# Six residual buffers, a closing norm in four pinned steps, and a bias added by an accumulating DMA

## The chip, the cores and the metric

The kernel runs on one core of a Trainium2 chip. A core has a matrix engine (TensorE, "PE" in the profile, with its weight loads as "PEld"), a vector engine (VectorE, "DVE"), an engine for activation functions (ScalarE, "ACT"), a general engine (GpSimd, "POOL"), and a queue engine that only issues DMAs (SyncE, "SP"). Each takes its own instructions in a fixed order and waits on semaphores for the others. The metric is the time of one execution on the device, in microseconds (us); lower is better.

## The reference

Two layers work on x of 32 examples of 512 rows of 256 columns, with a 512x512 adjacency matrix for each example. All arithmetic is float32.

```python
x = x + L0_gnn(layernorm(x), adj)
x = x + L0_ffn(layernorm(x))
x = x + L1_gnn(layernorm(x), adj)
x = x + L1_ffn(layernorm(x))

def L0_ffn(x):                       # 1024 features
    t = max over d of (x[:, d] + Wt[:, d]) + bt
    trop = s * max_k(t*sl_cvx + of_cvx) + (1-s) * min_k(t*sl_ccv + of_ccv)
    g = sigmoid(x @ Wg + bg)
    return (g * trop + (1-g) * gelu(x @ Wc + bc)) @ Wd + bd

def L1_gnn(x):                       # 4 heads of 64 columns
    h = x @ W
    att = softmax(leaky_relu(e_src + e_dst), masked by adj)
    out = relu(att @ h + bias) + h
    return (out - mean) / sqrt(var + 1e-6) * gamma + beta     # per head

def L1_ffn(x):                       # 8 heads, 64 slices
    sw = softmax((x @ W_x.T) @ W_slice.T / temperature)
    st = weighted means of x @ W_fx.T over the slices sw
    ot = a short two-directional scan over the 64 slice tokens, gated, RMS-normed
    return (ot spread back by sw) @ out_w.T + out_b
```

## The kernel before

The program is written for a scheduler. The source traces instructions in some order; the scheduler then simulates the program and gives each engine's instructions an order of their own: a later instruction that the simulation finds ready sooner can be put ahead of an earlier one. What it puts in an engine's queue is then fixed. `tc.keep_in_program_order(ins)` adds one edge to this: `ins` is not put ahead of the instruction that was traced just before it on the same engine. It adds no wait on the chip.

**Layer 0** (`layer0_sorted`, L98) runs from the start to about 2390 us. `convs` does the graph convolution, example by example. `feed_forwards` (L543) works on groups of 512 rows (32 groups in all): `sums` (L546) gathers the rows of a group with indirect DMAs (`xs`, L553), fetches rows of a table (`best`, L564; `rows`, L595) and takes their running maximum on VectorE (L598); `mixed` (L613) does the two matrix products with gelu and tanh and the piecewise linear parts; `down` (L645) multiplies by Wd and adds to `xg` (L654). At the end of `sums`, POOL adds the last bias `bd`, a constant of 128x256 in SBUF, to the four row tiles of `xg` (L609 to L610). The indirect DMAs are issued by POOL, from the same queue of instructions.

**Layer 1** (`layer1_plain`, L865) runs from there to the end. Two chains of Python generators are interleaved by hand:

- `attentions` (L1300): for each example b, `attention(b)` woven with `prepare(b + 1)`. `prepare` (L1136) loads the residual rows `x` with four indirect DMAs (L1142), issues the adjacency copy for b+2 (L1085), norms and transposes them, multiplies by W (`hp`, L1171), and makes `hv`, `mine`, `other` and `ht` from the product (L1174 to L1179). `mine` is turned by a TensorE transpose (`minep`, L1183) and goes through DRAM to every partition (`own`). `attention` (L1204) walks 8 turns of (head pair, row tile), weighs ahead of itself on VectorE (`att`, L1201) and multiplies on TensorE (`avp`, `adp`); it then divides, adds a bias by an accumulating DMA (L953) and leaves a generator `norm` (L1274) in `unfinished`. The steps of `norm` of example b are taken inside the turns of example b+1, at L1245. Its last step adds to the residual (L1296) and marks the example `attended`.
- `mixer(g)` (L1565), for pairs of examples: `slices` of both (softmax rows `sw`, products `yTp`, L1310), `tokens`, `scan` (L1375: a long chain of small products and vector work), and `unslice` (L1554: `outp`, and the store of the result, L1562).

The driver (L1581) steps the mixer; each yield of the mixer carries a number, which times `PACE` gives the number of attention steps to take next. If an attention step yields True, `prepare` is blocked, and the saved-up credit is dropped. `slices(b)` takes attention steps by itself for as long as b is not `attended`. `prepare(b)` is blocked until example b - `AHEAD_X` is stored, since the residual tile `x` has `AHEAD_X` buffers; it is held from `prepare` to `unslice`. `TURNS`, `STEPS` and `WANTED` count the yields of an attention, of `prepare`, and of a mixer's numbers.

All biases of layer 1 are kept in DRAM (`added`) and added by accumulating DMAs from POOL (`add_rows`, L951).

Of the kernel before, what the change touches and what calls it, by code (L numbers as in the profile page):

```python
# [8 lines left out]
F32 = mybir.dt.float32  # L9
# [5 lines left out]
ALU = mybir.AluOpType  # L15
# [4 lines left out]
P = 128  # L20
# [77 lines left out]
def layer0_sorted(tc, ident, eps, x, adj, w, x2s, ranks, over, following):  # L98
# [29 lines left out]
    with ExitStack() as ctx:  # L128
# [11 lines left out]
        bias = const("bias", [P, D], w["bias"].partition_broadcast(P))  # L140
        bd = const("bd", [P, D], w["bd"].partition_broadcast(P))
        wc = cst.tile([P, DC, FFN], F32, tag="wc", name="wc")
# [31 lines left out]
        for c in range(CT // P):  # L174
            nc.gpsimd.affine_select(below[:, c, :], below[:, c, :], pattern=[[1, CT]], compare_op=ALU.is_gt,
                                    fill=0.0, base=-c * P, channel_multiplier=-1)

        table = dr.tile([D, FFN], F32, tag="table", name="table", bufs=1)
        least = dr.tile([2, D], F32, tag="least", name="least", bufs=1)
# [363 lines left out]
        def feed_forwards():  # L543


            def sums(s, g):  # L546
# [57 lines left out]
                for c in range(DC):  # L604
# [3 lines left out]
                                        ALU.is_gt)  # L608
                for t in range(NT):  # L609
                    nc.gpsimd.tensor_add(xg[:, t, :D], xg[:, t, :D], bd)  # L610
                got[s, g] = xg, xnT, best
# [253 lines left out]
def layer1_plain(tc, ident, eps, x2s, ranks, adj, w, out, over, ps):  # L865
# [22 lines left out]
    AP = AH // 2  # L888
    TURNS = AP * NT + 6
    STEPS = 11  # L890
    WANTED = 68
    AHEAD = 3
    ATT = 2 * (AHEAD + 2) + AP + 1
    HW = P // AH
    AHEAD_X = 2 * GB + 1
    PACE = 1.04 * GB * (TURNS + STEPS) / WANTED

# [3 lines left out]
    with ExitStack() as ctx:  # L901
# [234 lines left out]
        def prepare(b):  # L1136
# [29 lines left out]
            other = sb.tile([P, NT, AH], F32, tag="other", name=f"other{b}")  # L1166
            mine = sb.tile([P, AH, NT], F32, tag="mine", name=f"mine{b}")
            for t in range(NT):
                ph = psum("any", f"hp{b}_{t}")
                for c in range(DC):  # L1170
                    nc.tensor.matmul(ph[:, : AH * (HO + 2)], xnT[:, c, t * P : (t + 1) * P], wa[:, c, :],  # L1171
                                     start=c == 0, stop=c == DC - 1)
                d = ph[:, AH * HO : AH * HO + AH]
                nc.scalar.activation(hv[:, t, :, HO], d, AF.Exp)  # L1174
                nc.vector.tensor_mul(hv[:, t, :, :HO], ph[:, : AH * HO].rearrange("p (h e) -> p h e", h=AH),
                                     hv[:, t, :, HO:].to_broadcast([P, AH, HO]))
                nc.scalar.activation(mine[:, :, t], ph[:, AH * (HO + 1) : AH * (HO + 2)], AF.Exp, scale=1.0 - SLOPE)
                nc.scalar.activation(other[:, t, :], d, AF.Exp, scale=SLOPE - 1.0)
                nc.scalar.copy(ht[:, t, :], ph[:, : AH * HO])  # L1179
                yield  # L1180

            pt = psum("any", f"minep{b}")
            nc.tensor.transpose(pt[: AH * NT, :P], mine.rearrange("p h t -> p (h t)"), ident)  # L1183
            row = sb.tile([AH * NT, P], F32, tag="turned", name=f"turned{b}", bufs=1)
# [19 lines left out]
        def attention(b):  # L1204
# [21 lines left out]
            for i, (q, j) in enumerate(turns):  # L1226
# [17 lines left out]
                yield  # L1244
                if unfinished and i not in (0, 3):  # L1245
                    next(unfinished[0], None)
                    yield
                    if i > 3:
                        unfinished.pop()
# [24 lines left out]
        def norm(b, av):  # L1274

            _, ht, _, _, _ = ready[b]
            xt = xs[b]
            NG = NT * AH
            flat = av.rearrange("p t h e -> p (t h e)")
            rows = av.rearrange("p t h e -> p t (h e)")  # L1280
            heads = av.rearrange("p t h e -> p (t h) e")
            nc.vector.scalar_tensor_tensor(flat, flat, 0.0, ht.rearrange("p t e -> p (t e)"), ALU.max, ALU.add)
            mu = sb.tile([P, 2, NG], F32, tag="mu", name=f"mu{b}")
            nc.vector.tensor_reduce(mu[:, 0, :], heads, AX.X, ALU.add)
            nc.vector.tensor_scalar_mul(mu[:, 0, :], mu[:, 0, :], 1.0 / HO)
            nc.vector.tensor_sub(heads, heads, mu[:, 0, :].unsqueeze(2).to_broadcast([P, NG, HO]))
            sq = ht.rearrange("p t (h e) -> p (t h) e", e=HO)
            nc.scalar.activation(sq, heads, AF.Square)
            yield
            nc.vector.tensor_reduce(mu[:, 1, :], sq, AX.X, ALU.add)  # L1290
            nc.vector.tensor_scalar(mu[:, 1, :], mu[:, 1, :], 1.0 / HO, 1e-6, ALU.mult, ALU.add)
            nc.gpsimd.tensor_tensor(mu[:, 1, :], mu[:, 1, :], eps[:, 1:2].to_broadcast([P, NG]), ALU.pow)  # L1292
            nc.vector.tensor_mul(rows, rows, gamma.unsqueeze(1).to_broadcast([P, NT, AH * HO]))
            yield
            nc.vector.tensor_mul(heads, heads, mu[:, 1, :].unsqueeze(2).to_broadcast([P, NG, HO]))
            nc.vector.tensor_add(xt, xt, rows)  # L1296
            del ready[b]
            attended.add(b)
# [76 lines left out]
        def scan(g, uT):  # L1375
# [161 lines left out]
            rms = sb.tile([P, GB], F32, tag="rms", name=f"rms{g}")  # L1537
            nc.vector.tensor_scalar(rms, pm[:, :GB], 1.0 / DI, LN_EPS, ALU.mult, ALU.add)
            nc.gpsimd.tensor_tensor(rms, rms, eps[:, 1:2].to_broadcast([P, GB]), ALU.pow)
# [691 lines left out]
```

## Time and profile before

| What | Value |
|---|---|
| Runs, median of 3 (lowest to highest) | 4513.17 us (4503.5 to 4514.52) |
| The profiled execution, its own time | 4515.02 us |
| Its span, first to last instruction | 4513.3 us |
| Mean granted TensorE clock | 0.94 |
| Busy, VectorE | 3204.0 us of the span |
| `bd` additions L610, POOL | 128, 108.2 us, mean 850 ns |
| `av<-added` L953, POOL's time to issue | 32, 28.1 us, mean 878 ns |
| Closing norm, L1282, L1284, L1286, L1293, L1295, L1296 (VectorE) | 32 of each, 1.21 to 1.23 us each |
| Power of the closing norm, L1292 (POOL) | 32, mean 3.18 us |
| Square of the closing norm, L1288 (ScalarE) | 32, mean 1.06 us |
| Gathered rows `x`, L1142 (POOL) | 128, mean 1.03 us to issue |

How to read it: busy time says how full an engine is, idle time that ends on a releaser says what it waited for. In the views of waits a line names the waiting engine, tile and line, the engine, tile and line that released it, the total in us, how often, and the longest. In a timeline a line gives the start, the length, the engine, the line of the source, the operation, the tiles, and in brackets the idle time of the engine just before and what ended it. Averages over the whole span mix two layers with different limits, so the stretch of the layer in question is looked at by itself.

### The profile page before, as it was taken

The page shows a single profiled execution, that of the slowest core. Times are in us where ns is not written, and L with a number is a line of the kernel's source. Part 1 is how long each engine was busy: PE and PEld are TensorE (multiplying, and loading weights), DVE is VectorE, ACT ScalarE, POOL GpSimd, SP SyncE. Part 2 cuts the span into 40 slices and gives each one's busy share as a digit, 9 for nine tenths or more (in the row PEclk, how much of TensorE's full clock was granted, in tenths as well). Part 3 has the DMA queues.
Part 4 walks back from the last instruction along what each step waited for, and adds up shares of the span by engine and source line. Part 5 has one row for each costly group of instructions (what it writes and reads, how often), then busy time and mean ns, then how long its engine had stood idle before and what let it go on. Part 6 is the DMA issues. An engine that isn't in the chain of part 4 may idle for free.

```text
span 4513.3 us, 56135 instructions
## 1 busy us (share of the span) xinstructions
PE 3933.4 (87%) x19799; PEld 2468.0 (55%) x19799; DVE 3204.0 (71%) x6909; ACT 2198.0 (49%) x4305; POOL 1570.2 (35%) x2069
## 2 busy tenths in 40 slices
PE   5567898899988999889997999898998898989987
PEld 4454565656656656555553555555555455555555
DVE  6678888897788877867765766656666666666663
ACT  3345565556565665545663444344444443444433
POOL 2356544664446554444313122222211222222110
PEclk8778999999999999989998999999999999999998
DMA  5546543664446643564315233333322333333210
GB/s 129 160 142 224 184 140 110 206 202 154 135 129 206 194 141 109 169 216 160 129 59 117 52 76 79 80 80 68 83 68 62 73 80 80 80 70 76 62 38 20
DMA packets 301248, 524.04 MB, mean 116 GB/s; under 512 B 104823, under 2 KB 180227, under 8 KB 300956
## 3 DMA queue, kind: packets, MB, share of 16 engines
q0 software_dynamic: 117120, 383.06, 30.6%
q1 hardware_dynamic: 183836, 137.30, 10.4%
q8 instruction: 158, 2.59, 0.2%
q14 instruction: 134, 1.10, 0.1%
HBM read 463.11 MB, written 73.95 MB: 119 GB/s over the span
## 4 chain that ended last, share of the span: by engine, by line
PE 32%; DVE 31%; DMA 15%; issue 9%; POOL 8%; ACT 4%; SPq 1%; DVEq 0%; POOLq 0%; ACTq 0%
DVE acc L637 4%; PE clsp L623 4%; PE po L652 4%; DMA av<-added 3%; PE yTp L1339 3%; PE gatep L623 3%; PE outp L1559 3%; POOL mu L1292 2%; DMA rows<-table,xs 2%; DMA out<-x 2%; DMA rows<-table,tops 2%; DVE best L598 2%; PE oTp L1527 2%; DVE att L1201 2%; PE avp L1237 2%
## 5 line engine op out<-in xcount | busy, mean ns | idle before, releaser
L623 PE MATMUL clsp<-xnT,wc 128*128 128x512 f32 x1024 | 524.8, 631 | 46.7 <-ACT cls L625 34.4
L623 PE MATMUL gatep<-xnT,wg 128*128 128x512 f32 x1024 | 496.8, 605 | 9.3 <-ACT gate L625 9.3
L652 PE MATMUL po<-wd,acc 128*128 128x256 f32 x2048 | 457.3, 382 | 8.4 <-DVE acc L641 5.9
L652 PEld LDWEIGHTS po<-wd,acc 128*128 128x128 f32 x2048 | 389.2, 192 | 75.2 <-issue 9.6
L1201 DVE SCALAR_TENSOR_TENSOR att<-own,other,mask 128x512 f32<-128x512 f32 x512 | 358.3, 737 | 12.8 <-DMA own<-ownd 12.8
L598 DVE SCALAR_TENSOR_TENSOR best<-rows,xs,best 128x1024 f32<-128x1024 f32 x212 | 272.6, 1288 | 126.8 <-ACT best L592 79.5
L637 DVE SCALAR_TENSOR_TENSOR acc<-past,fld,acc 128x512 f32<-128x512 f32 x448 | 344.6, 772 | 23.8 <-ACT past L636 16.0
L1237 PE MATMUL avp<-att,hv 128*32 128x512 f32 x2048 | 333.0, 601 | 7.2 <-DVE att L1201 7.2
L1339 PE MATMUL yTp<-sw,x 128*128 128x512 f32 x512 | 262.1, 666 | 88.0 <-DVE sw L1334 88.0
L623 PEld LDWEIGHTS gatep<-xnT,wg 128*128 128x128 f32 x1024 | 196.8, 196 | 253.3 <-issue 203.5
L632 ACT ACTIVATE acc<-tz,fld 128x512 f32<-128x512 f32 x256 | 198.7, 776 | 279.1 <-PE tz L630 247.4
L636 ACT ACTIVATE past<-tz,fld 128x512 f32<-128x512 f32 x448 | 291.5, 693 | 79.3 <-DVE acc L637 77.7
L595 POOL DMA_INDIRECT rows<-table,xs x212 | 251.5, 1186 | 170.3 <-DVE best L598 117.3
L623 PEld LDWEIGHTS clsp<-xnT,wc 128*128 128x128 f32 x1024 | 183.9, 200 | 185.9 <-issue 114.1
L434 PE MATMUL pm<-h,adj 128*128 128x258 f32 (+1 forms) x1024 | 182.9, 326 | 103.9 <-DVE keep L427 42.6
L1327 PE MATMUL lgp<-wsl,x4T 128*128 128x512 f32 x512 | 241.3, 617 | 22.4 <-ACT x4T L1131 22.4
L625 ACT ACTIVATE gate<-gatep,fld 128x512 f32<-128x512 f32 x256 | 175.4, 685 | 146.4 <-PE gatep L623 124.0
L553 POOL DMA_INDIRECT xs<-rows_of,order x128 | 156.7, 1225 | 215.3 <-DVE acc L637 93.3
L1339 PEld LDWEIGHTS yTp<-sw,x 128*128 128x128 f32 x512 | 104.9, 214 | 227.5 <-DVE sw L1334 126.2
L1559 PE MATMUL outp<-v,swT 128*128 128x256 f32 x1024 | 226.2, 379 | 0.0
L434 PEld LDWEIGHTS pm<-h,adj 128*128 128x128 f32 x1024 | 152.8, 215 | 129.2 <-issue 73.4
L625 ACT ACTIVATE cls<-clsp,fld 128x512 f32<-128x512 f32 x256 | 176.0, 687 | 95.3 <-PE clsp L623 58.8
(593 smaller groups left out, 8550.7 us busy)
## 6 DMA issues: line engine op xcount, KB each, us to landing
adj<-in_adj POOLq DMA_DIRECT2D x128, 256.0 KB
x<-added POOLq DMA_DIRECT2D x64, 512.0 KB
own<-ownd SPq DMA_DIRECT2D x128, 256.0 KB
rows_of<-keep SPq DMA_DIRECT2D x32, 550.0 KB
x<-in_x SPq DMA_DIRECT2D x32, 512.0 KB
x2s<-xs SPq DMA_DIRECT2D x32, 512.0 KB
short<-in_adj POOLq DMA_DIRECT2D x32, 512.0 KB
av<-added POOLq DMA_DIRECT2D x32, 512.0 KB
```

What stands on the lines that cost most here:

```text
L434: nc.tensor.matmul(pm[:, : c1 - c0], a[:, i, t * P : (t + 1) * P], h[:, i, c0:c1], start=i + c0 == 0, stop=i + 1 == NT and c0 > 0)
L595: nc.gpsimd.indirect_dma_start(out=row, out_offset=None, in_=table, in_offset=bass.IndirectOffsetOnAxis(ap=idxs[:, k : k + 1].bitcast(U32) ...
L598: nc.vector.scalar_tensor_tensor(m, row, vals[:, k : k + 1], m, ALU.add, ALU.max)
L623: nc.tensor.matmul(pf, wf[:, c, f * P : (f + 1) * P], xnT[:, c, :], start=c == 0, stop=c == DC - 1)
L625: nc.scalar.activation(o, pf, fn, bias=fld[:, f, bf : bf + 1], scale=1.0 if fn == AF.Gelu else 0.5)
L636: nc.scalar.activation(r, z, AF.Relu, bias=fld[:, f, AT + b : AT + b + 1])
L637: nc.vector.scalar_tensor_tensor(y, r, fld[:, f, CH + b : CH + b + 1], y, ALU.mult, ALU.add)
L652: nc.tensor.matmul(po[:, i, :], acc[f][:, t * P : (t + 1) * P], wd[:, f, :], start=f == 0, stop=f == FC - 1)
L1201: nc.vector.scalar_tensor_tensor(e, own[h], other[:, j, h : h + 1], mask[:, j, :], ALU.max, ALU.mult)
L1237: nc.tensor.matmul(pv[p][k * HW : (k + 1) * HW, :], hv[:, j, h, e : e + HW], weighed[b, h, j], **ends)
L1339: nc.tensor.matmul(py, xn[:, t, c * P : (c + 1) * P], sw[:, t, :], start=t == 0, stop=t == NT - 1)
L1559: nc.tensor.matmul(po[:, :D], swT[:, k, t * P : (t + 1) * P], v[:, k, :], start=k == 0, stop=k == KC - 1)
```

## The change

- `AHEAD_X` is 2 * GB + 2 = 6 instead of 5: a sixth buffer for the residual tile, and `prepare(b)` is blocked only until b - 6 is stored.
- `norm` has four steps instead of three: the square on ScalarE is a step of its own. The steps are taken after turns 1, 2, 3 and 6 of the next example, where the three steps were taken after turns 1, 2 and 4. Four of its instructions, the first of each step on its engine, are kept in program order. `TURNS` counts one more.
- In `scan` there is one more yield before `rms`, and `rms` is kept in program order. `WANTED` counts one more.
- In `prepare`, the product of `hv` on VectorE reads the copy `ht` in SBUF instead of the PSUM tile, and is traced one row tile later. The transpose of `mine` is kept in program order.
- In layer 0, `bd` lives in DRAM, repeated for the four row tiles, and is added to a group's rows by one accumulating DMA from POOL instead of four POOL additions. The SBUF constant is gone.

```diff
-        bd = const("bd", [P, D], w["bd"].partition_broadcast(P))
...
+        bd = dr.tile([NT, D], F32, tag="bd", name="bd", bufs=1)
+        nc.sync.dma_start(bd, w["bd"].partition_broadcast(NT))
...
-                for t in range(NT):
-                    nc.gpsimd.tensor_add(xg[:, t, :D], xg[:, t, :D], bd)
+                nc.gpsimd.dma_start(xg[:, :, :D], bd.partition_broadcast(P), accum_op=ALU.add)
...
-    TURNS = AP * NT + 6
+    TURNS = AP * NT + 7
     STEPS = 11
-    WANTED = 68
+    WANTED = 69
...
-    AHEAD_X = 2 * GB + 1
+    AHEAD_X = 2 * GB + 2
...
+            def values(t):
+                nc.vector.tensor_mul(hv[:, t, :, :HO], ht[:, t, :].rearrange("p (h e) -> p h e", h=AH),
+                                     hv[:, t, :, HO:].to_broadcast([P, AH, HO]))
+
             for t in range(NT):
...
                 nc.scalar.activation(hv[:, t, :, HO], d, AF.Exp)
-                nc.vector.tensor_mul(hv[:, t, :, :HO], ph[:, : AH * HO].rearrange("p (h e) -> p h e", h=AH),
-                                     hv[:, t, :, HO:].to_broadcast([P, AH, HO]))
                 nc.scalar.activation(mine[:, :, t], ph[:, AH * (HO + 1) : AH * (HO + 2)], AF.Exp, scale=1.0 - SLOPE)
                 nc.scalar.activation(other[:, t, :], d, AF.Exp, scale=SLOPE - 1.0)
                 nc.scalar.copy(ht[:, t, :], ph[:, : AH * HO])
+                if t:
+                    values(t - 1)
                 yield
 
+            values(NT - 1)
+
             pt = psum("any", f"minep{b}")
-            nc.tensor.transpose(pt[: AH * NT, :P], mine.rearrange("p h t -> p (h t)"), ident)
+            tc.keep_in_program_order(
+                nc.tensor.transpose(pt[: AH * NT, :P], mine.rearrange("p h t -> p (h t)"), ident))
...
-                if unfinished and i not in (0, 3):
+                if unfinished and i in (1, 2, 3, 6):
                     next(unfinished[0], None)
                     yield
                     if i > 3:
...
-            nc.vector.scalar_tensor_tensor(flat, flat, 0.0, ht.rearrange("p t e -> p (t e)"), ALU.max, ALU.add)
+            tc.keep_in_program_order(
+                nc.vector.scalar_tensor_tensor(flat, flat, 0.0, ht.rearrange("p t e -> p (t e)"), ALU.max, ALU.add))
...
             sq = ht.rearrange("p t (h e) -> p (t h) e", e=HO)
-            nc.scalar.activation(sq, heads, AF.Square)
-            yield
-            nc.vector.tensor_reduce(mu[:, 1, :], sq, AX.X, ALU.add)
+            yield
+            tc.keep_in_program_order(nc.scalar.activation(sq, heads, AF.Square))
+            yield
+            tc.keep_in_program_order(nc.vector.tensor_reduce(mu[:, 1, :], sq, AX.X, ALU.add))
             nc.vector.tensor_scalar(mu[:, 1, :], mu[:, 1, :], 1.0 / HO, 1e-6, ALU.mult, ALU.add)
             nc.gpsimd.tensor_tensor(mu[:, 1, :], mu[:, 1, :], eps[:, 1:2].to_broadcast([P, NG]), ALU.pow)
             nc.vector.tensor_mul(rows, rows, gamma.unsqueeze(1).to_broadcast([P, NT, AH * HO]))
             yield
-            nc.vector.tensor_mul(heads, heads, mu[:, 1, :].unsqueeze(2).to_broadcast([P, NG, HO]))
+            tc.keep_in_program_order(
+                nc.vector.tensor_mul(heads, heads, mu[:, 1, :].unsqueeze(2).to_broadcast([P, NG, HO])))
             nc.vector.tensor_add(xt, xt, rows)
...
             rms = sb.tile([P, GB], F32, tag="rms", name=f"rms{g}")
-            nc.vector.tensor_scalar(rms, pm[:, :GB], 1.0 / DI, LN_EPS, ALU.mult, ALU.add)
+            yield 1
+            tc.keep_in_program_order(
+                nc.vector.tensor_scalar(rms, pm[:, :GB], 1.0 / DI, LN_EPS, ALU.mult, ALU.add))
```

## The prediction

> **What bounds the kernel now.** I read the page first, then the engines' busy time over layer 1's steady stretch, then TensorE's waits there, then all waits and the timelines of one period.
>
> The page's first part says TensorE is the fullest engine, but not full:
>
> ```profile
> PE 3933.4 (87%) x19799; PEld 2468.0 (55%) x19799; DVE 3204.0 (71%) x6909; ACT 2198.0 (49%) x4305; POOL 1570.2 (35%) x2069
> ```
>
> Layer 1's mixer repeats every 129.9 us (the first `yTp` of a pair of examples starts at 3268.41 and the next pair's at 3398.27). Over 14.2 such periods, from 2500 to 4340 us (columns: length, busy time of PE, PEld, DVE, ACT, POOL, clock, DMA share, GB/s):
>
> ```profile
> 2500.00:4340.00 1840.00, 1674.99 (x10525) 988.58 (x10527) 1194.32 (x2744) 794.32 (x1862) 384.07 (x416) 0.96 0.33 73
> ```
>
> TensorE idles 1840.0 - 1675.0 = 165 us, 11.6 a period, and nothing else is above 65%. So the stage is bound by TensorE plus the waits that end on it. These are, in the same stretch (us, times, longest):
>
> ```profile
> PE yTp L1339 <- DVE sw L1334: 87.4, 21, 7.5
> PE lgp L1327 <- ACT x4T L1131: 21.5, 15, 3.4
> PE minep L1183 <- ACT mine L1177: 17.1, 14, 1.3
> PE oTp L1527 <- ACT yT L1521: 10.2, 14, 0.7
> PE yp L1509 <- DVE mix L1502: 8.4, 13, 0.6
> ```
>
> More than half is one stall a period: TensorE waits for the softmax rows `sw`. Why they are late is read in the timeline of POOL and VectorE, 3376 to 3395:
>
> ```profile
> 3383.88 1.06 POOL L1142 DMA_INDIRECT x<-x2s,ranks  x1 [3.84 <-DMA out<-x]
> ...
> 3389.30 2.96 POOL L1292 TENSOR_TENSOR mu<-mu,eps 128x16 f32<-128x16 f32 x1
> ```
> ```profile
> 3392.30 1.22 DVE L1295 TENSOR_TENSOR av<-av,mu 128x1024 f32<-128x1024 f32 x1 [9.53 <-POOL mu L1292]
> ```
>
> The row loads of an example ahead (L1142) wait for the output store that frees their buffer. The power of the closing norm (L1292) stands behind them on POOL though its input was ready at 3381.4. VectorE stands at L1295 for 9.53 us with the sixteen `sw` instructions of the next example behind it. TensorE runs dry at 3391.1. Over 2600 to 4300 us the same kind of stall, an engine standing at an instruction fed late by another, shows as:
>
> ```profile
> ACT ht L1288 <- DVE av L1286: 317.6, 27, 20.7
> ACT mine L1177 <- DVE hv L1175: 148.5, 27, 12.1
> ```
> ```profile
> DVE av L1295 <- POOL mu L1292: 151.2, 27, 9.9
> DVE rms L1538 <- PE msp L1535: 92.9, 13, 7.9
> ```
>
> These do not add up on the path; they say which instructions stand in front of others.
>
> [...] after the 6.12 us stall before 3268.41 the granted clock is 0.50 until past 3272, and those sixteen `yTp` matmuls take 9.28 us against 7.21 for the sixteen at 3297.99. A long stall costs 2.07 us more than itself. [...] L598 takes 1.28 us alone and 1.58 to 1.75 beside POOL's two-input additions. [...]
>
> **The change part by part.** The sum is against the profiled execution, 4515.0 us (span 4513.3); the median of the runs, 4513.2, is 1.8 lower, so results are moved by that.
>
> 1. *Six residual buffers.* The buffer of example b is free once b-6 is stored, not b-5. Now b=17 needs the store of 12 and b=18 that of 13, both just made; with six, 17's is a period old and 18's is the first of the pair. L1142's waits (59.4 us, 26 times) should go. Two things follow. POOL reaches L1292 earlier: four loads at 1.25 us and the adjacency copy 0.61 are 5.6 us from 3375, so the power could run from 3381.4 instead of 3389.3, 7.9 us sooner. And the hand-written interleave is no longer stopped: a blocked `prepare` yields True and sets the credit to zero, so attention steps meant for the scan are now pushed in a lump ahead of the next `slices`. x += rows (L1296) ends at 3330.15 and its reader begins at 3330.73: no lead at all. Six buffers let up to one example of lead grow.
> 2. *Norm in four steps, `rms` after a yield, both pinned.* No instruction is added. L1288, L1295 and L1538 are queued behind what was traced before them; in the trace that is attention multiplications (0.74 us each) and `sw` work that was ready. What is behind a pinned instruction still waits for it, but for less. The price: the last quarter moves from turn 4 to turn 6, later by two turns, four L1201 x 0.74 = 3.0 us of VectorE and 24 matmuls, about 2.6 us. Cover is the lead of part 1.
>    Parts 1 and 2 together: the `yTp` stall is 6.2 us a period (87.4/14); in the period above VectorE was free from 3382.8 and the rows take 7.7 us (3265.05 to 3272.78 one period earlier), so nearly all can go. I take 5.0 x 14 = 70, and of the clock's 2.07 x 14 = 29 I take 24. With L1288 no longer holding ACT (18.8 us at 3377, the `x4T` copies behind it), `lgp`'s 21.5 gives 12.
> 3. *`values` from `ht`, one tile later.* Four VectorE products per example move from PSUM to SBUF; L1175 is 0.42 us and no SBUF row of that shape is in the trace, but L639 (both in SBUF, 0.70 for 512 columns) against L1265 (one in PSUM, 0.68) says the same price: 128 x 0.02 = under 3 us either way, hidden in VectorE's 35% idle. ACT's `mine` no longer waits for it, and with the pinned transpose `minep` (17.1) I take 12.
> 4. *New waits and the end.* A denser queue gets stalls of its own; the trace can't show them. Bounds 0 and 4 us a period (then the gain is mostly given back); I take 1.5 x 14 = 21. More lead ends attention sooner, so more of the mixer at the end runs without filler: there it idles 4.29 + 5.73 us already before 4376. I take 10.
> 5. *Layer 0's bias.* Out: 128 POOL additions of 0.85 us, 108.2. In: 32 accumulating DMAs; `av<-added` issues in 0.88, so 28 us of POOL. Net 80 us of POOL's 1120 there; POOL isn't the bound. Relief for VectorE: L637's mean is 0.772 against 0.74 undisturbed, 0.03 x 448 = 14 us, and L598's excess about 11; if 40% is L610's, 10 us. Against it: 32 x 512 KB more through POOL's queue (4.4% of its 383 MB). `av<-added` takes 5.2 us to land; gathers behind it are late by 0 to 5.2. At 1436 us two gathers took 10.08 us with the DMA engines full and TensorE idle for 5.19, so it is not always covered. Behind the DMA's own wait for the last `xn` read stand gathers as well; the additions waited there too (190 us, 43 times). Bounds -25 and +166; I take +10 for traffic, -10 for VectorE: 0. The constant's own move is one 4 KB copy, covered by the 301 us before its first use (L610's first start).
>
> Sum: 70 + 24 + 12 + 12 = 118 gained, 21 + 10 given back: 87. 4515.0 - 87 = 4428; as a median 4426.
>
> **Rivals.**
> - *The interleave gains more:* the lead fills the scan's bubbles as well (`oTp`, `yp`, `rnp`: 25 us) and no new waits come: 118 + 21 = 139, so 4374 to 4390; take 4385. For it: 165 us of idle and no other full engine. Against: those bubbles are single-chain waits of 0.6 us.
> - *Nothing to tell (4513):* the stall is only moved, the power's chain (3.3 us on POOL after a DMA) sets the period wherever it stands. Against: its input was ready 7.9 us before it ran.
> - *Slower, the late quarter:* if the lead doesn't grow (pace 4% above need), each `slices` starts 3.0 us later with no cover: 32 x 3.0 = 96, and the `yTp` stall stays. With `minep` and `lgp` gained: 4513 + 96 - 24 = 4585. It decides once the quarter's delay exceeds the buffer's gain; the 0.6 us between L1296 and its reader speak for it, the unblocked `prepare` against.
> - *Slower, layer 0's queue:* the accumulating DMA in front of gathers, in full: 166 - 87 = +79, 4592. It flips the sign from 2.7 us a group. Its transfer is real; most gathers have four buffers of lead against it.
>
> **How the numbers follow.** Forecast 0.55 (its own range 4395 to 4465), gains more 0.20, nothing 0.07, late quarter 0.10, layer 0 0.08. About 0.3%, 13.5 us, is what can be told from no change here. Faster 0.75, same 0.07, slower 0.18. The range from 4370 to 4540 leaves out the far part of the two slower cases and a little below.
>
> **What would show it.** Right: no L1142 wait for the store; L1295's and L1538's waits under a third; `yTp`'s under 25 us; sixteen `yTp` at 7.2; TensorE above 94% in the steady stretch; a period near 123 us; layer 0 ending within 15 us of before. Wrong: L1296 directly ahead of its reader still, `lgp` or `yTp` waits as before; ACT waiting at L1164 for a later reduction; gathers or POOL standing at the new DMA, layer 0 longer.

## The result and the profile after

The change makes the kernel barely faster: 4500.77 us median of 20 runs (4490.82 to 4519.19) against 4510.6 us of the kernel before on the same chips (4495.61 to 4527.49, 20 runs). The ratio is 0.998, with a 95% interval of 0.9971 to 0.999. The forecast was 4426.

The busy times of the kernel after, on its page:

```profile
PE 3943.5 (88%) x19799; PEld 2480.2 (55%) x19799; DVE 3180.0 (71%) x6909; ACT 2199.5 (49%) x4308; POOL 1515.7 (34%) x1973
```

Where the 19.6 us between the two profiled spans (4513.3 and 4493.7) come from is read from the first and last start of two tiles, `po` (the end of layer 0) and `outp` (layer 1's last product):

| Stretch | Before | After | Difference |
|---|---|---|---|
| Start to the last `po` of layer 0 | 2386.3 | 2356.2 | -30.1 |
| From there to the first `outp` | 202.5 | 211.1 | +8.6 |
| First `outp` to last `outp` | 1914.9 | 1914.4 | -0.5 |
| Last `outp` to the end | 9.6 | 12.0 | +2.4 |

So layer 0, where nothing was expected, gives all of the gain, and layer 1, where 87 us were expected, gives none: from the last `po` to the end it takes 2127.0 us before and 2137.5 after. The stretch from 2500 to 4340 us of the kernel after (length, busy time of PE, PEld, DVE, ACT, POOL, clock, DMA share, GB/s), and TensorE's largest waits in it:

```profile
2500.00:4340.00 1840.00, 1695.90 (x10575) 1008.26 (x10574) 1209.20 (x2737) 796.61 (x1849) 389.38 (x406) 0.96 0.33 71
```
```profile
PE yTp L1530 <- DVE y L1525: 30.2, 14, 2.3
PE yTp L1350 <- DVE sw L1345: 28.5, 34, 2.4
PE yp L1520 <- DVE mix L1513: 16.9, 14, 1.5
PE gp L1490 <- ACT cpad L1465: 14.0, 12, 1.2
PE yTp L1350 <- ACT sw L1339: 13.7, 3, 5.5
PE oTp L1538 <- ACT yT L1532: 9.4, 14, 0.7
PE qp L1504 <- ACT ht L1182: 9.4, 12, 1.1
```

The long stall for `sw` went from 87.4 to 42.2 us (28.5 + 13.7), and `lgp`'s wait from 21.5 to 3.1. In their place the scan waits: for `y` (30.2, new), `yp` twice as long as before, `gp` and `qp` new. TensorE is busy 20.9 us longer than before in this stretch, or 92% of it, but holds only 50 more matmuls (10575 against 10525, 8 us at the same pace). So more than half of the idle time that went (20.9 us) came back as busy time for the same work (12.9 us). The granted clock shows why. Two neighbouring windows of 4 us at the end of one scan, before and after:

```profile
3466.10:3470.10 4.00, 4.00 (x23) 2.96 (x23) 1.66 (x5) 2.44 (x4) 0.00 (x0) 1.00 0.00 0
3470.10:3474.10 4.00, 3.36 (x40) 2.78 (x39) 2.88 (x7) 2.88 (x14) 0.91 (x1) 1.00 0.06 10
```
```profile
3447.70:3451.70 4.00, 1.89 (x33) 1.76 (x32) 4.00 (x7) 1.09 (x4) 0.90 (x1) 0.93 0.28 23
3451.70:3455.70 4.00, 1.70 (x7) 1.33 (x8) 2.00 (x6) 1.97 (x5) 0.00 (x0) 0.50 1.03 266
```

After the change TensorE has little beside the scan there. Counted from the pair's first `outp`, the attention products (`avp` and `adp` together) take 9.2 us from 99 to 109 us before and 0.6 after, as means of 14 periods; from 60 to 80 us, among the second example's `yTp`, they take 1.6 before and 10.9 after. The filler, work that TensorE does beside the scan's chain, went to the waits for `sw`, some 30 us earlier. In the bare scan, the second pair of windows, TensorE is busy 1.89 and 1.70 us of 4.00, and the granted clock is 0.50 in the last one. Counted from the first `outp` to 4340 us, the clock fell to 0.50 before the change 12 times after 3.4 us in which TensorE was busy 0.03 us at most (the long stall); after the change it fell so once. At the scan's end it fell 7 times before, for 3.4 us each (TensorE busy 1.39 to 1.56 us of the 3.41 ahead), and 13 times after, at `yp`, for 6.8 us or more each (1.77 to 1.91 us of 3.41). From 2500 to 4340 us, the time lost to the clock, (1 - granted clock) x time, is 64.9 us before and 75.8 after: 10.9 us more, which can be most of the 12.9.

What VectorE and then TensorE do in this scan of the kernel after (timelines):

```profile
3448.36 0.69 DVE L1513 TENSOR_TENSOR mix<-mix,decay 128x512 f32<-128x512 f32 x1
3448.97 1.22 DVE L1306 TENSOR_TENSOR av<-av,mu 128x1024 f32<-128x1024 f32 x1
3450.10 0.42 DVE L1170 TENSOR_TENSOR hv<-ht,hv 128x256 f32<-128x256 f32 x1
3450.43 1.22 DVE L1307 TENSOR_TENSOR x<-x,av 128x1024 f32<-128x1024 f32 x1
3451.57 0.69 DVE L1524 TENSOR_TENSOR y<-y,yp 128x512 f32<-128x512 f32 x1
```
```profile
3449.20 1.87 PE L1520 MATMUL yp<-xk,mix 64*64 64x64 f32 x32 [1.48 <-DVE mix L1513]
3453.33 1.09 PE L1530 MATMUL yTp<-ident,y 128*128 128x128 f32 x4 [2.26 <-DVE y L1525]
```

The norm's last quarter (L1306, L1307) and a product of `hv` stand between the scan's `mix` and its `y`, mostly while `yp` runs: `yp` was done at 3451.07, and `y` (L1524) started 0.5 us later. TensorE got `y` for `yTp` at 3453.33. So most of this 2.26 us wait is the scan's own chain, bare of filler, and not the norm's work in front of it.

POOL still waits for the store. From the views of all engines' waits, 2600 to 4300 us, before and then after:

```profile
POOL x L1142 <- DMA out<-x: 59.4, 26, 4.2
```
```profile
POOL xpad L1406 <- ACT sp L1440: 403.0, 13, 32.1
...
POOL x L1142 <- DMA out<-x: 79.2, 9, 9.8
...
POOL x L1142 <- DVE x L1574: 42.5, 4, 11.4
```

The loads L1142 wait 79.2 us for the store and 42.5 us for L1574, the sum that is stored; it was 59.4 us before. At the start of layer 1, where 8.6 us are lost, `avp` waits 19.0 us for the first weighings, 7.2 before.

### The profile page after: what moved, and what is told of

The parts are those of the page before. It is cut to its first block, busy times and chain, and to the rows that moved or that the text cites. A ratio compares the mean times of both kernels' runs of the same rounds, so it can differ in the third digit from the quotient of the medians.

```text
span 4493.7 us, 56074 instructions
## 1 busy us (share of the span) xinstructions
PE 3943.5 (88%) x19799; PEld 2480.2 (55%) x19799; DVE 3180.0 (71%) x6909; ACT 2199.5 (49%) x4308; POOL 1515.7 (34%) x1973
## 4 chain that ended last, share of the span: by engine, by line
PE 38%; DVE 19%; DMA 13%; issue 8%; ACT 8%; POOL 6%; SPq 0%; POOLq 0%; DVEq 0%; ACTq 0%
PE clsp L623 4%; PE avp L1245 4%; PE gatep L623 4%; PE yTp L1350 4%; PE po L652 3%; PE outp L1572 3%; DVE acc L637 3%; DMA own<-ownd 3%; DMA rows<-table,xs 2%; DVE best L599 2%; DMA best<-table,xs 2%; DMA x<-x2s,ranks 2%; PE adp L1250 2%; POOL x L1142 1%; PE oTp L1538 1%
## 5 line engine op out<-in xcount | busy, mean ns | idle before, releaser
L637 DVE SCALAR_TENSOR_TENSOR acc<-past,fld,acc 128x512 f32<-128x512 f32 x448 | 332.9, 746 | 27.6 <-ACT past L636 19.6
L1350 PE MATMUL yTp<-sw,x 128*128 128x512 f32 x512 | 252.5, 628 | 43.6 <-DVE sw L1345 29.1
L1142 POOL DMA_INDIRECT x<-x2s,ranks x128 | 144.7, 1131 | 208.9 <-DMA out<-x 79.2
```

Source lines behind the costliest of these rows:

```text
L637: nc.vector.scalar_tensor_tensor(y, r, fld[:, f, CH + b : CH + b + 1], y, ALU.mult, ALU.add)
L1350: nc.tensor.matmul(py, xn[:, t, c * P : (c + 1) * P], sw[:, t, :], start=t == 0, stop=t == NT - 1)
```

## The experiments

Ratios are against the kernel before on the same chip, with their 95% interval. Each edit lets the scheduler sort the rest anew, so ratios of parts need not multiply.

### Layer 0 alone, layer 1 alone

`e1_l0_only` is the kernel before with this:

```diff
-                for t in range(NT):
-                    nc.gpsimd.tensor_add(xg[:, t, :D], xg[:, t, :D], bd)
+                nc.gpsimd.dma_start(xg[:, :, :D], bd.partition_broadcast(P), accum_op=ALU.add)
```

> The kernel before with one edit: layer 0's last bias comes by an accumulating DMA instead of four POOL additions a group. Theory A (layer 0 alone carries the result): layer 0's last po product ends some 30 us earlier, as it does with the whole change (2356 against 2386 us), layer 1 is untouched, ratio 0.993 to 0.994, about 4482. Theory B (layer 0's gain came from something else in the change, or is given back at once): layer 0 as before, ratio 0.998 to 1.002. My prediction's term was 0.

Measured: 4489.51 us, ratio 0.9959 (0.9944 to 0.9975). Layer 0's last `po` starts at 2357.6. The median gains less than theory A said, but its mechanism stands: layer 0 ends 28.7 us earlier, and layer 1 takes 2128.5 us, as before. `e16_no_bias` leaves the bias of layer 0 out:

```diff
-                for t in range(NT):
-                    nc.gpsimd.tensor_add(xg[:, t, :D], xg[:, t, :D], bd)
```

> The kernel before without the last bias of layer 0: the four POOL additions a group are left out and nothing takes their place, so this part of the computation is missing. If the gain of layer 0's DMA is the relief of POOL and VectorE and the DMA itself is free: the same 0.994 to 0.9975 as with the DMA. If the DMA's traffic takes back some of the relief (my term of +10): 0.991 to 0.994. If the gain came from another order of layer 0's instructions: 0.998 to 1.002.

Measured: 4476.72 us, 0.9932 (0.9917 to 0.9948); the last `po` starts at 2349.9. So without the additions layer 0 ends some 36 us earlier (2386.3 - 2349.9). How much of this the DMA takes back is not shown: in the 14 profiles of kernels here with the DMA, layer 0 ends between 2338.8 and 2366.9 (mean 2355.5), in the five with the additions between 2373.8 and 2386.3 (mean 2381.7). The DMA's gain of some 26 us is clear of that spread; a difference of 8 us between two profiles is not. The groups of VectorE and POOL in layer 0 (0 to 2390 us; busy, mean ns, idle before and what ended it), before and then `e1_l0_only`:

```profile
L637 DVE SCALAR_TENSOR_TENSOR acc<-past,fld,acc 128x512 f32<-128x512 f32 x448 | 344.6, 772 | 23.8 <-ACT past L636 16.0 <-DVE shifta L46 0.3
L610 POOL TENSOR_TENSOR xs<-xs,bd 128x256 f32<-128x256 f32 x128 | 108.2, 850 | 191.0 <-ACT xn L574 190.0
```
```profile
L637 DVE SCALAR_TENSOR_TENSOR acc<-past,fld,acc 128x512 f32<-128x512 f32 x448 | 332.2, 744 | 30.2 <-ACT past L636 21.8 <-DVE deg L439 0.4
L610 POOL DMA_DIRECT2D xs<-bd x32 | 44.6, 1393 | 85.5 <-ACT xn L575 61.5 <-issue 13.2 <-ACT cls L625 10.3
```

VectorE's `acc` gives 12.4 us, and L598's two groups 1.7 and 4.8 (272.6 to 270.9, 163.3 to 158.5): 18.9 us. The trace of before shows where they were lost: the 46 `acc` that overlap an addition of L610 take 1015 ns in the median, the 139 beside no POOL instruction 745; of L598, 25 overlap one and take 1583 ns, and 108 beside no POOL instruction 1283. POOL stands 105 us less at L610 in front of its gathers. The instructions of layer 0 also came out in a slightly other order. These runs don't separate the three.

`e2_l1_only` is the whole change with `bd` added on POOL as before.

```diff
-                nc.gpsimd.dma_start(xg[:, :, :D], bd.partition_broadcast(P), accum_op=ALU.add)
+                for t in range(NT):
+                    nc.gpsimd.tensor_add(xg[:, t, :D], xg[:, t, :D], bd)
```

> The whole change without its layer 0 part. Theory A: layer 1's edits bring nothing in the steady stretch and cost some 9 us at its start, ratio 1.002 to 1.005, 4515 to 4530, and layer 0 ends at 2386. Theory B: layer 1's edits do gain and only meet a loss elsewhere, ratio 0.985 to 0.997. My prediction's terms for layer 1 were -87: ratio 0.981.

Measured: 4516.96 us, 1.0019 (1.0007 to 1.0031). Layer 1's edits together lose a little; theory A holds in sign, at the low end of its size. Layer 0 ends at 2374, 12 us earlier than before, though nothing in it was edited; layer 1 alone takes 2135.7 us against 2127.0.

### The parts of layer 1 alone

`e3_six_only`:

```diff
-    AHEAD_X = 2 * GB + 1
+    AHEAD_X = 2 * GB + 2
```

> The kernel before with six residual buffers and nothing else. My prediction's step 1: the loads' waits for the store go, the power of the closing norm runs some 8 us sooner, the stall of yTp behind it shrinks from 87 us to under 30, ratio 0.985 to 0.990. Theory A: the engines' orders come out nearly as before, so the attention's lead doesn't grow; the store's wait only turns into less waiting on POOL in some of the periods, ratio 0.996 to 1.001, and the yTp stall stays above 60 us. Theory C (the loads' wait wasn't for the buffer but for the queue of stores, so it stays): ratio 0.999 to 1.001 and L1142's waits as before.

Measured: 4484.93 us, 0.9947 (0.9929 to 0.9966), between the two forecasts. POOL at the start of one pair's output, in this kernel:

```profile
3355.95 1.08 POOL L1142 DMA_INDIRECT x<-x2s,ranks  x1 [1.45 <-DMA out<-x]
...
3370.11 0.99 POOL L1142 DMA_INDIRECT x<-x2s,ranks  x1 [8.44 <-DMA out<-x]
3371.40 0.96 POOL L1142 DMA_INDIRECT x<-x2s,ranks  x1 [0.30 <-issue]
3372.67 0.96 POOL L1142 DMA_INDIRECT x<-x2s,ranks  x1 [0.31 <-issue]
3373.93 0.95 POOL L1142 DMA_INDIRECT x<-x2s,ranks  x1 [0.30 <-issue]
3374.91 2.94 POOL L1292 TENSOR_TENSOR mu<-mu,eps 128x16 f32<-128x16 f32 x1
```

The loads run 11 and 25 us after the pair's first `outp`, as before (11 and 26), and the power L1292 behind them. Only the example loaded is another: counting the loads, these are the 19th and 20th (b = 18, 19), where the kernel before loads 17 and 18 at that place. A load depends on nothing but its buffer, so the scheduler puts it ahead in POOL's queue until it stands at the store that frees the buffer. With one buffer more it stands at the same store for one example later. The wait doesn't go, it grows (from 2600 to 4300 us; 59.4 before):

```profile
POOL x L1142 <- DMA out<-x: 89.5, 21, 9.4
```

What six buffers buy is data early: the odd examples' loads now start 125 us ahead of `x3T` instead of 13. But TensorE had waited only 2.1 us for `x3T`, so this is not shown to be where the 0.5% comes from; in the trace `sw`'s wait falls from 84.5 to 65.0 us, and the time lost to the clock from 78.5 to 61.4, first to last `outp`.

`e4_norm_only` is the kernel before with the norm's four pinned steps at turns 1, 2, 3 and 6, and the pinned `rms`:

```diff
-                if unfinished and i not in (0, 3):
+                if unfinished and i in (1, 2, 3, 6):
...
+            yield 1
+            tc.keep_in_program_order(
+                nc.vector.tensor_scalar(rms, pm[:, :GB], 1.0 / DI, LN_EPS, ALU.mult, ALU.add))
```

> The kernel before with the closing norm in four pinned steps and the pinned rms, five residual buffers, nothing else. Theory A: it is the pins and the new turns that move the stall: yTp's wait for the softmax rows falls below 40 us, waits inside the scan (y, gp, qp, yp) grow by about as much, ratio 0.998 to 1.004. Rival of my prediction (the late quarter without a lead costs 3 us an example): ratio 1.015 to 1.021. Theory D (the pins gain and the six buffers give it back): ratio 0.985 to 0.995.

Measured: 4628.56 us, 1.0261 (1.0241 to 1.028), beyond all three. The stall for `sw` is 10.2 us, so the steps do end it. But with five buffers an odd example's rows arrive when its norm is due, POOL waits 160 us for stores, and TensorE waits 94 us (4.0 to 9.6 a pair) for `x3T`. With the sixth buffer this wait is gone, in the whole change and without the product as well (`e12_no_val` below).

`e5_val_only` has the product of `hv` from `ht` and the pinned transpose:

```diff
-                nc.vector.tensor_mul(hv[:, t, :, :HO], ph[:, : AH * HO].rearrange("p (h e) -> p h e", h=AH),
-                                     hv[:, t, :, HO:].to_broadcast([P, AH, HO]))
...
+                if t:
+                    values(t - 1)
```

> The kernel before with only the product of hv read from ht, one row tile later, and the pinned transpose of mine. My prediction's step 3: minep's 17 us of waits fall below 6 and 12 us are gained, ratio 0.997. Theory A2 (the late product stands in front of the scan's vector work): minep's waits fall, but waits inside the scan (qp, yp, y) grow by as much or more, ratio 1.000 to 1.005.

Measured: 4505.86 us, 0.9994 (0.9983 to 1.0004): nothing. `minep`'s wait fell from 16.8 to 4.3 as expected, and `sw`'s rose from 84.5 to 93.6.

### Combinations without the held loads

`e9_l0_six` is layer 0's DMA and six buffers (the diffs of `e1_l0_only` and `e3_six_only`).

> Layer 0's DMA and six buffers, nothing else. If the two parts add up, 0.9959 x 0.9947 = 0.9906, 4468 us. If they don't (the 0.9951 of these two with the product from ht is then no loss by that product): 0.993 to 0.997.

Measured: 4448.9 us, 0.9897 (0.9882 to 0.9911): they add up, and these two parts are 0.8% better than the whole change. `e6_no_norm` adds the product and the transpose to these two (the diff of `e5_val_only`).

> The whole change without the closing norm's four pinned steps and the pinned rms: layer 0's DMA, six buffers and the product from ht stay. Theory E (the norm's steps and pins are what costs, the rest adds up): the ratios of layer 0's DMA alone and of six buffers alone give 0.9959 x 0.9947 = 0.9906, times 0.997 to 1.003 for the product: 0.987 to 0.994, about 4467. Theory F (the pinned steps are what makes the other edits work, as they end the long yTp stall): ratio 0.996 to 1.000, and yTp's wait for the softmax rows is back above 60 us.

Measured: 4489.1 us, 0.9951 (0.9934 to 0.9969). Neither theory fits: the ratio lies between, and `sw`'s wait is 78.6 us. The product and the pinned transpose cost 0.5% here. `e12_no_val` is the whole change with the product from PSUM and the transpose free:

```diff
-                if t:
-                    values(t - 1)
+                nc.vector.tensor_mul(hv[:, t, :, :HO], ph[:, : AH * HO].rearrange("p (h e) -> p h e", h=AH),
+                                     hv[:, t, :, HO:].to_broadcast([P, AH, HO]))
```

> The whole change with hv's product from PSUM and without the pinned transpose, as before. Theory V (the product from ht, behind ScalarE's copy, is what stands in the scan's way): the waits for qp and gp, 8.7 and 20.8 us, fall below 5 each and the ratio is 0.990 to 0.995. Theory E2 (the norm's turns do it): 0.997 to 1.002, as the whole change.

Measured: 4518.66 us, 1.0052 (1.0037 to 1.0067). Beside the norm's steps the same two gain 0.7%, so theory V falls, and the loss is larger than E2 said. Three kernels vary the steps:

```diff
e7_no_pins
-            tc.keep_in_program_order(nc.scalar.activation(sq, heads, AF.Square))
+            nc.scalar.activation(sq, heads, AF.Square)
...
e8_turn4
-                if unfinished and i in (1, 2, 3, 6):
+                if unfinished and i in (1, 2, 3, 4):
...
e11_no_rms
-            yield 1
-            tc.keep_in_program_order(
-                nc.vector.tensor_scalar(rms, pm[:, :GB], 1.0 / DI, LN_EPS, ALU.mult, ALU.add))
+            nc.vector.tensor_scalar(rms, pm[:, :GB], 1.0 / DI, LN_EPS, ALU.mult, ALU.add)
```

> The whole change with its steps, turns and yields as they are, but nothing of the norm nor rms kept in program order. If the pins cost (theory P: a pinned instruction that waits stops the scan's work behind it): ratio 0.988 to 0.994, the waits for y, gp and qp fall below 30 us together. If the late turns cost (theory T: the last quarter after turn 6 delays whoever reads x): ratio 0.997 to 1.006. If the pins pay (theory F): slower than the whole change, above 1.006, with a yTp stall of over 60 us.

> The whole change with the norm's last quarter after turn 4, as before, instead of turn 6; its pins stay. Theory T (the late turn costs): ratio 0.988 to 0.994. Theory P (the pins cost wherever the quarter is): 0.997 to 1.003, with the scan's waits about as in the whole change. Against both: one turn after the reduction, the power's 3.2 us on POOL may not be done, and VectorE stands at the pinned product (L1306) for it again: yTp's wait for the softmax rows above 60 us and 1.002 to 1.010.

> The whole change without the extra yield before rms and its pin. Theory E2 (the norm's turns move filler out of the scan, rms adds nothing): 0.996 to 1.001. Theory R (rms, late on VectorE, is what costs): 0.990 to 0.995.

Measured: `e7_no_pins` (all five pins of norm and `rms` gone) 4556.15 us, 1.011 (1.0091 to 1.0129); `e8_turn4` 4537.25 us, 1.0065 (1.0045 to 1.0085), with `sw`'s wait back at 103 us; `e11_no_rms` 4487.99 us, 0.9982 (0.997 to 0.9993). At these turns the pins pay (though the stall for `sw` is 44 us without them, not the 60 of theory F), with the pins turn 6 pays, and `rms` does nothing beside them. So none of these three, taken back by itself, mends the change.

### Held loads

`e3_six_only` says that the power stands behind loads put ahead. `e10_loads_held` tests it: `e9_l0_six` with

```diff
-                nc.gpsimd.indirect_dma_start(
+                tc.keep_in_program_order(nc.gpsimd.indirect_dma_start(
                     out=xt[:, t, :], out_offset=None, in_=x2s[b // SEG],
```

> Layer 0's DMA and six buffers, and the gathered loads L1142 kept in program order, so that they aren't put ahead on POOL to the store that frees their buffer. Theory H (a load put ahead in POOL's queue stands at the store with any number of buffers, and the closing norm's power behind it): L1142's waits for the store, 89.5 us with six buffers alone, fall below 15, the power runs some 8 us sooner in one example of two, the product behind it (L1295) waits under 80 instead of 153, yTp's wait for the softmax rows falls from 65 to under 25, and the ratio is 0.978 to 0.986. Rival I (the power isn't what ends the stall, the softmax chain of the next example is late anyway): the power runs sooner, yTp's wait stays above 50, ratio within 0.003 of the kernel without the hold. Rival J (a held load comes late for its own norm): PE waits at x3T and ratio above 0.995.

Measured: 4408.24 us, 0.9792 (0.9774 to 0.9809). All of theory H came. VectorE's wait for the power and TensorE's for `sw`, from 2600 to 4300 us, in `e3_six_only`:

```profile
DVE av L1295 <- POOL mu L1292: 149.0, 27, 10.0
```
```profile
PE yTp L1339 <- DVE sw L1334: 65.0, 22, 6.0
```

and in `e10_loads_held`:

```profile
DVE av L1295 <- POOL mu L1292: 14.2, 15, 3.0
```
```profile
PE yTp L1339 <- DVE sw L1334: 2.5, 6, 0.4
```

The loads' wait for a store is gone from the list, the power of the pair's first example starts 23 to 26 us after the first `outp` instead of 29 to 32, and the periods are 119 to 127 us, where I had forecast 123 for the change itself. `e14_hold_five` holds the loads with five buffers:

```diff
-    AHEAD_X = 2 * GB + 2
+    AHEAD_X = 2 * GB + 1
```

> Layer 0's DMA and the held loads, with five buffers. If six buffers matter only because a load was put ahead to its store: with the hold the fifth buffer is freed late only for one example of two, whose load still stands at the store of the pair's first, at a time when no power waits: 0.979 to 0.985, within 0.004 of six. If the sixth buffer is what lets the held load go without the store's wait: 0.985 to 0.995, with L1142 waiting for the store and the yTp stall back in part.

Measured: 4391.47 us, 0.9749 (0.9731 to 0.9767), the best of all kernels here and better than either answer. Once the loads are held the sixth buffer isn't needed. Why five are even better is only in part seen: `sw`'s wait is longer than with six (23.1 us against 2.5), but from first to last `outp` 34.1 us are lost to the clock against 56.3, and layer 1's first `outp` comes 8 us sooner after layer 0. `e13_whole_hold` is the whole change with the same hold.

> The whole change with the gathered loads held in program order on POOL. If the loads that stand at the store are what keeps the whole change from gaining: their waits (79 and 53 us) go, ratio 0.978 to 0.986, as with the hold on layer 0's DMA and six buffers. If the norm's late quarter and pins cost by themselves, by taking filler out of the scan: the loads' waits go, but the waits for y, yp, gp and qp (85 us) and the half clock at the scan's end stay, ratio 0.990 to 0.998.

Measured: 4477.94 us, 0.9926 (0.9907 to 0.9945): the second answer, the steps cost by themselves. `e15_hold_val` is `e10_loads_held` with the diff of `e5_val_only`, and `e18_hold_minep6` with its pinned transpose only:

```diff
-            nc.tensor.transpose(pt[: AH * NT, :P], mine.rearrange("p h t -> p (h t)"), ident)
+            tc.keep_in_program_order(
+                nc.tensor.transpose(pt[: AH * NT, :P], mine.rearrange("p h t -> p (h t)"), ident))
```

> Layer 0's DMA, six buffers, held loads, and also the product from ht and the pinned transpose. My prediction's step 3, with the long stall gone: minep's wait falls from 20 to under 6, ratio 0.975 to 0.978. Against it, as without the hold, where this edit took 0.9897 to 0.9951: 0.980 to 0.986, with new waits for yTp and vp.

> Layer 0's DMA, six buffers, held loads and only the pinned transpose of mine; the product of hv from PSUM as before. If the late product is what cost 1% on top of the held loads: 0.976 to 0.981, minep's wait near 20 us. If the pinned transpose did (TensorE's queue held behind it): 0.985 to 0.991.

Measured: 4460.58 us, 0.9892 (0.9873 to 0.991), and 4428.14 us, 0.9825 (0.9806 to 0.9845). The second lies between its two answers: the transpose takes about a third of the loss, the late product the rest. TensorE and then VectorE in `e15_hold_val`:

```profile
PE vp L1557 <- DVE rms L1546: 61.4, 13, 6.4
```
```profile
3323.01 0.75 DVE L1209 SCALAR_TENSOR_TENSOR att<-own,other,mask 128x512 f32<-128x512 f32 x1 [8.60 <-DMA own<-ownd]
3323.68 0.15 DVE L1546 TENSOR_SCALAR rms<-msp 128x2 f32<-128x2 f32 x1
```

A weighing of the next example was put ahead of `rms` and waits 8.60 us for its rows; a 0.15 us instruction behind it holds TensorE. That is what the pinned `rms` is against: with it, below, `vp` waits 5.2 us for `rms`. `e17_no_norm_hold` is `e13_whole_hold` with the norm as before:

```diff
-    TURNS = AP * NT + 7
+    TURNS = AP * NT + 6
...
-                if unfinished and i in (1, 2, 3, 6):
+                if unfinished and i not in (0, 3):
```

> The whole change with held loads, but the closing norm's three steps, turns and freedom as before: six buffers, layer 0's DMA, the product from ht, the pinned transpose and the pinned rms stay. Theory K (the product from ht let VectorE put an attention weighing that waits for its own rows ahead of rms, so that TensorE waited 61 us for rms, and the pinned rms is what mends that): vp's wait for rms below 10 us, ratio 0.975 to 0.982, and the norm's new steps are what the whole change with held loads (0.9926) loses. If the norm's steps cost nothing once the loads are held: 0.990 to 0.995, as that one. If the product costs by itself: 0.987 to 0.991, as without the pinned rms.

Measured: 4406.82 us, 0.9781 (0.9765 to 0.9798): theory K. The norm's steps alone separate 0.9926 from 0.9781. From the first `outp` of the first pair to that of the last, 15 periods, `e13_whole_hold` and then `e17_no_norm_hold`:

```profile
2580.26:4456.58 1876.32, 1738.67 (x10699) 1031.07 (x10696) 1218.79 (x2772) 814.11 (x1869) 394.77 (x415) 0.96 0.32 70
```
```profile
2566.12:4379.68 1813.56, 1677.77 (x10725) 1003.30 (x10724) 1207.12 (x2778) 761.51 (x1839) 405.25 (x416) 0.98 0.33 73
```

TensorE idles 137.7 us in one and 135.8 in the other. So of the difference of 62.8 us, 60.9 are busy time for the same work. The time lost to the clock is 81.9 us against 29.0, so the clock makes up to 52.9 of them; the other 8 stay open. Once the loads are held, the norm's steps cost busy time, most of it clock, and not idle time.

## Why the prediction was wrong

Two steps failed, the first and the second. What each cost is read from layer 1 alone, last `po` to the end, which agrees within 5 us in the three kernels that leave it as it was (2124.3 to 2128.5). The whole change takes 2137.5 us there; with the loads held 2118.8, 19 less (`e13_whole_hold`); with the norm as before too 2042.2, another 77 less (`e17_no_norm_hold`). That this is 85 us under before, where 87 were forecast, is in good part luck: `sw` still costs it 29.7 us, and from first to last `outp` it loses 50 us less to the clock, where 24 were forecast.

1. *Six residual buffers*, "L1142's waits (59.4 us, 26 times) should go" and "the power could run ... 7.9 us sooner": this step failed in its mechanism. A buffer doesn't take away the wait of a load that the scheduler puts ahead to its store (89.5 us with six buffers alone), and the power stayed behind it. Holding the load in program order, not adding the buffer, made it true (`e10_loads_held`). The claim that a blocked `prepare` held up the interleave was wrong too. Stepping through the driver's generators, `prepare` is never blocked, with five buffers or with six, and the steps taken at each yield are the same. The traces agree: from `x3T` to `x4T` of one example it takes 161 or 175 us before and 156 or 174 with six buffers alone. So no lead grew from them.
2. *The norm's steps and pins*: this step failed in what it left out, and it is the larger part. Of the 70 us of `yTp` stall that I counted, 45 went (87.4 to 42.2). The 24 us of clock came with the other sign: 10.9 us more lost. I had counted only the half clock behind the long stall, which did go (12 falls to one), not the one that a bare scan would bring (13 falls at `yp`). `lgp` came and was more than forecast (21.7 to 3.9 us from first to last `outp`, for 12).
3. *The product from `ht`*: its own price was as said, and `minep`'s wait fell by 9 us where I took 12. But with the transpose alone it gave nothing, with six buffers and without the pinned `rms` the two cost 0.5% to 1.0%, and beside the norm's steps they gained 0.7%. What they move in the queues counts, not the product's 0.42 us.
4. *New waits*, taken as 21 us with bounds of 0 and 4 us a period: `y`, `gp` and `qp` alone are 53.6 us in the stretch, 3.8 a period, and `yp` adds 8.5. At 4.4 us a period the term was above its upper bound. What I had missed is that the attention work is a fixed amount, so that what fills one gap opens another. The end of the kernel cost 2.4 of the 10 us set for it.
5. *Layer 0*, taken as 0: the trace shows -30.1 us, and the DMA alone a ratio of 0.9959. Relief of VectorE was 18.9 us against 10. The cost of the traffic, put at 10, is too small to be told here. What I left out of the sum was POOL's 190 us at L610 in front of gathers, of which 105 went; how much of that shortened layer 0 is not shown. Issue cost 1.39 us each, not 0.88.

Of the rivals, "nothing to tell" (4513) came nearest, in part by luck: layer 0's 30 us were in no sum. Its mechanism, a stall only moved, is right for layer 1, though not through the power's chain. The late quarter without lead was real too: with the other steps and the pins it cost layer 1 some 125 us with five buffers (`e4_norm_only`) and 34 with six (`e12_no_val`).

Left open: which part of the norm's edit (steps, turns or pins) costs once the loads are held. Pins at the old turns, and a lower or higher pace of the interleave, were not tried.

## What to carry to other kernels

Before adding a buffer for a wait, ask whether the order in the queue is fixed by that wait: a DMA that a scheduler may put ahead can stand at the next buffer just as well, with whatever is behind it (here 59.4 us of waits with five buffers, 89.5 with six). Hold the DMA where it is needed. And where filler work fills TensorE's gaps, count the filler: moving it to the longest stall leaves another place bare. Here that was the scan's end: TensorE was busy there for 1.77 to 1.91 us of 3.41, the granted clock fell to 0.50 behind it 13 times, and the time lost to the clock rose by 10.9 us although the long stall's falls had gone.

## What the hardware showed that was not expected

The clock halved without a long stall. In the scan of the kernel after, TensorE idled from 3447.73 to 3449.20 (1.48 us), worked for 1.87 us, and the granted clock fell from 1.00 to 0.50 at about 3451.1; it came back at about 3457.9. In the 3.4 us before the fall TensorE was busy for 1.90 us, more than half; before the fall at 3265.93 of the kernel before, in the long stall, it was busy for 0.00 of 3.41. So these traces have to be read for stretches of low share, not only for long gaps.

The traces of the kernels before and after show more. In both, all changes of the granted clock lie whole multiples of 3.41 us apart. Take such windows at full clock, from the first to the last `outp`, by the share of time that TensorE was busy in them. In the two traces together the clock fell after 33 of 34 with less than half, after 14 of 24 with 50 to 60%, and after 1 of 966 with more. Busy time alone doesn't settle the middle group: before the change none of 7 fell, after it 14 of 17. Of these 14, 13 hold the scan's `yp`, small products of 64x64; whether small products count for less was not tried.
